# Four edits in the SSD stage of a four-layer convolution and state-space kernel: mask of the decays one slot earlier, pair scaling as one tensor-tensor operation, first convolution pass of B and C as scalar-tensor-tensor, turned B earlier

## The chip, the cores and the metric

The kernel runs on one core of one Trainium2 chip. A core has five engines with queues of their own: TensorE (PE in the profile, its weight loads PEld), VectorE (DVE), ScalarE (ACT), GpSimd (POOL) and SyncE (SP), which issues most transfers. The metric is the device time of one execution in microseconds, the median of several runs. All data are float32.

## The reference

An image batch x of shape (4, 96, 64, 64) goes through four layers one after the other. Layers 0 and 2 are selective-scan Mamba blocks with a fusion and a batch norm. Layer 3 is a 7x7 depthwise convolution with a layer norm and a two-layer perceptron. The change touches only layer 1, a state-space dual (SSD) layer:

```
xn = rmsnorm(x over channels) * norm_w
xs = four orders of the 4096 positions: rows, rows reversed, columns, columns reversed   # 16 sequences
z, xBC, dt = split(xs @ in_proj_w.T)              # 192, 192 + 128 + 128, 3
dt = softplus(dt + dt_bias)
xBC = silu(conv_b + causal 4-tap convolution of xBC along the sequence)
xh, B, C = split(xBC)                             # 3 heads of 64; 128 states
# by chunks; dAc = cumulative sum of dt * A in the chunk
y  = ((C B^T) * exp(dAc_s - dAc_t, s >= t) * dt) @ xh        # within the chunk
y += (C @ previous state) * exp(dAc)                         # what is carried in
state = exp(dAc_last) * state + (exp(dAc_last - dAc) * dt * xh)^T B
y  = rmsnorm((y + D * xh) * silu(z)) * gnorm_w
out = mean over the four orders of (y @ out_proj_w.T) + x
```

## The kernel before, in words

`program` runs the layers in order: `mamba_fusion`, `ssd`, `mamba_fusion`, `convnext`. The SSD stage is the class `Ssd`. For each of the 4 images it walks two orders (o: rows, columns) in two directions (r: forward, backward), and each of these 16 sequences in four blocks of 1024 positions (`BLK`), so there are 64 blocks. A block is eight chunks of 128 positions (`QB`, `Q`); there are 512 chunks.

`run` (L1401) is one loop over slots n, one slot for a chunk. In every slot each step is done for another chunk: `at(lag)` is the chunk n - lag, so `at(-4)` is four chunks ahead. What the steps are:

- `sums_to` (L1206) fetches, for a pair of chunks, the rows of cumulative decays from DRAM into dr, 128 times over the partitions, on SP.
- `mask_of` (L1219) adds a mask to dr on GpSimd and writes seg (128 x 3 x 128), for which there are six buffers. `decay` (L1227) takes three exponentials of seg on ScalarE. `weights` (L1240) multiplies seg by C B^T on VectorE.
- `inputs` (L1246) makes three scaled copies xs of x on GpSimd. `state` (L1266) multiplies xs by turned B on TensorE, `decayed` (L1275) scales the state before on GpSimd, and `update` (L1285) adds the two on VectorE.
- `carried` (L1294) and `within` (L1303) are the two matmuls that give y; `decayed_out` (L1311, VectorE), `skip` (L1320, GpSimd) and `gate` (L1324, VectorE) add them up and multiply by the gate z.
- `square` (L1334) and `scale` (L1339) make the inverse root mean square on ScalarE, for a pair of chunks in ssq. `scaled` (L1346) multiplies the pair yz by it on GpSimd, with two operations of 128 x 192. `by_channels`, `turned`, `project` and `finish` transpose the pair, project it and add it to the output X.

The projections and convolutions of a block are made by `front` (L1066), which returns a plan: a list of actions by age, four ages for a slot, begun 15 slots (`AHEAD`) before the block's first chunk. The first chunk's slot has age 60, and each slot calls the plan at four points (`fill(0)` to `fill(3)`), so two plans are usually under way. Actions of the plan:

- `channels` and `biased` (L1091, L1099): x by three matmuls with the convolution folded into the weights, and the bias added on VectorE.
- `project` (L1105), `begin` (L1116), `convolve` (L1126): B or C, whose bank in PSUM then goes through four passes on VectorE, one tap each. The first pass, in `begin`, multiplies by a tap and adds the bias with a tensor-scalar operation that has two scalars per partition. The three others are scalar-tensor-tensor operations that add to the tile.
- `gates` and `gated` (L1132, L1143): z on TensorE and its copy on ScalarE, made in the forward direction and kept for the backward one. z has five buffers.
- `silu_x` at age 36 and `silu_bc` at 46, on ScalarE, with a load of the activation table before and after.
- `turned` (L1161) and `kept` (L1170): B of four chunks transposed on TensorE and copied to bt on ScalarE; for chunks 0 to 3 at ages 56 and 57, for chunks 4 to 7 at ages 57 and 58. `state` of the block's first chunk is issued at age 58, after the plan's actions of age 57.

x, B and C, z, and the transposes of B share three PSUM banks ("front"). The order of the work on TensorE, VectorE, ScalarE and GpSimd is the order in which `run` writes it: L1529 to L1534 tie each instruction of a slot to the one before it on its engine. Only SP's order is left to the framework. Preludes of the next sequence are spread over the slots: for the row order `rmsnorm` (L888, work on all engines), for the column order `turn` (L941), which copies xn transposed on GpSimd, eight copies of 96 x 512.

Of the kernel before, what the change touches and what calls it, by code (L numbers as in the profile page):

```python
# [18 lines left out]
F32 = mybir.dt.float32  # L19
AF = mybir.ActivationFunctionType  # L20
ALU = mybir.AluOpType
# [5 lines left out]
L = HH * WW  # L27
P = 128
# [28 lines left out]
DI = 192  # L57
DST = 128
NH = 3
HD = 64  # L60
CONV = DI + 2 * DST
Q = 128
NQ = L // Q
BLK = 1024
QB = BLK // Q
# [242 lines left out]
class Scan:  # L308
# [118 lines left out]
    def keep(self, g, i):  # L427
# [3 lines left out]
        else:  # L431
            self.fuse(g, i, xs, self.po)

    def run(self, steps, wts, front, first, later):


# [16 lines left out]
        for n in range(-LEAD, total + 26):  # L453
            start = len(traced)
            if (n + LEAD) % each == 0 and (step := (n + LEAD) // each + 1) < len(steps):
                fronts.append((n, front(step, made[step])))
# [104 lines left out]
def mamba_fusion(ctx: ExitStack, tc, k, src, dst, w):  # L561
# [99 lines left out]
    for _ in front(0, made):  # L661
        pass
# [83 lines left out]
class Ssd:  # L746
# [141 lines left out]
    def rmsnorm(self, b):  # L888
# [36 lines left out]
        def stored(n, g):  # L925
            self.store_row(rows, n, g["pd"])

        stages = (load, None, affine, residual, squared, mean, root, scaled, row, stored)
        for m in range(4 * NT + len(stages)):
            for n, g in enumerate(items):  # L930
# [135 lines left out]
    def front(self, b, o, r, blk, made, following):  # L1066

        nc, k = self.nc, self.k
        xn = self.xn[o]
        base = blk * BLK
        plan = {}

        def at(age, what, *args):
            plan.setdefault(age, []).append((what, args))

        held = {}  # L1080

        order = range(QB) if r == 0 else range(QB - 1, -1, -1)

        def start():
            made["x"], made["bc"] = [], []
            if r == 1:
                made["z"] = self.z[blk]
            held["pk"] = self.pk
            self.pk = None

        def channels(m):  # L1091
            p = held["x", m] = self.bank("front")[:, :DI]
            for i in range(3):
                nc.tensor.matmul(  # L1094
                    p, lhsT=held["pk"][:, i, ds(order[m] * Q, Q)], rhs=self.conv[:, i],
                    start=(i == 0), stop=(i == 2),
                )

        def biased(m):  # L1099
            half, i = divmod(m, HALF_X)  # L1100
            if i == 0:
                made["x"].append(self.work.tile([P, HALF_X, DI], F32, name=f"x{half}"))
            nc.vector.tensor_tensor(made["x"][half][:, i], held.pop(("x", m)), self.xbias, ALU.add)

        def project(i):  # L1105
            q, (m0, m1) = i % 2, PARTS[i // 2]
            t0, n = min(order[m0], order[m1 - 1]) * Q, (m1 - m0) * Q
            p = self.bank("front")
            nc.tensor.matmul(
                p[:, : n + 3], lhsT=self.inw[:C, 2 * DI + q * DST : 2 * DI + (q + 1) * DST],  # L1110
                rhs=xn[:C, ds(base + t0 + (0 if r == 0 else PAD), n + 3)], start=True, stop=True,
            )
            shifts = [p[:, ds(tap if r == 0 else 3 - tap, n)] for tap in range(4)]
            held["bc", i] = n, shifts

        def begin(i):  # L1116
            q, (n, shifts) = i % 2, held["bc", i]
            if q == 0:
                made["bc"].append(self.work.tile([P, 2, n], F32, name=f"bc{i // 2}"))
            out = made["bc"][i // 2][:, q]  # L1120
            held["bc", i] = out, shifts
            nc.vector.tensor_scalar(
                out, shifts[3], self.taps[:, q, 3:4], self.bcbias[:, q : q + 1], ALU.mult, ALU.add
            )

        def convolve(i, tap):  # L1126
            q, (out, shifts) = i % 2, held["bc", i]
            nc.vector.scalar_tensor_tensor(  # L1128
                out, shifts[tap], self.taps[:, q, tap : tap + 1], out, ALU.mult, ALU.add
            )  # L1130

        def gates(c):  # L1132
            if c == 0:
                made["z"] = self.z[blk] = self.work.tile([P, QB, DI], F32, name="z", bufs=L // BLK + 1)
            p = held["z", c] = self.bank("front")[:, : 2 * DI]
            for i in range(2):
                nc.tensor.matmul(
                    p[:, i * DI : (i + 1) * DI],
                    lhsT=xn[:C, ds(PAD + base + (c + i) * Q, Q)], rhs=self.inw[:C, :DI],
                    start=True, stop=True,  # L1140
                )

        def gated(c):  # L1143
            z = made["z"][:, c : c + 2]
            nc.scalar.copy(z.rearrange("p c n -> p (c n)"), held.pop(("z", c)))

        def silu(tiles):
            for n, t in enumerate(tiles):
                k.act.other(t, t, AF.Silu, back=(n == len(tiles) - 1))

        def silu_x():
            silu(made["x"] + [made["z"]] * (r == 0))

        def silu_bc():
            silu(made["bc"])

        def load():
            if following and following[:2] in self.ready:
                self.pk = self.stack(*following[1:])

        def turned(m):  # L1161
            if m == 0:
                made["bt"] = self.work.tile([P, QB, DST], F32, name="bt")
            p = held["bt", m] = self.bank("front")
            for i in range(4):
                nc.tensor.transpose(
                    p[:, i * Q : (i + 1) * Q], self.part_of(made, r, m + i)[:, 0], k.ident
                )

        def kept(m):  # L1170
            bt = made["bt"][:, m : m + 4]
            nc.scalar.copy(bt.rearrange("p c n -> p (c n)"), held.pop(("bt", m)))

        at(0, start)
        for m, age in enumerate(XAGES):
            at(age + 1, biased, m)
        for i, age in enumerate(BCAGES):
            at(age + 1, begin, i)
            for tap in range(3):
                at(age + 2 + tap, convolve, i, tap)  # L1180
        if r == 0:
            for i, age in enumerate(ZAGES):
                at(age + 1, gated, 2 * i)
        for m, age in enumerate(XAGES):
            at(age, channels, m)
        for i, age in enumerate(BCAGES):
            at(age, project, i)
        if r == 0:
            for i, age in enumerate(ZAGES):
                at(age, gates, 2 * i)  # L1190
        at(24, load)
        at(36, silu_x)
        at(46, silu_bc)
        for m in (0, 4):
            at(57 + m // 4, kept, m)
            at(56 + m // 4, turned, m)
        return plan

    @staticmethod
# [18 lines left out]

    def mask_of(self, g):  # L1219

        seg = g["seg"] = self.work.tile([P, NH, Q], F32, name="seg", bufs=6)
        self.nc.gpsimd.tensor_tensor(  # L1222
            seg, g["pair"]["dr"][:, ds(g["c"] % 2 * NH, NH)],
            self.mask[:, g["r"]].to_broadcast([P, NH, Q]), ALU.add,
        )
# [120 lines left out]
    def scaled(self, g):  # L1346

        yz, ssq = g["pair"]["yz"], g["pair"]["ssq"]
        for n in range(2):
            self.nc.gpsimd.tensor_scalar(yz[:, n], yz[:, n], ssq[:, n : n + 1], None, ALU.mult)  # L1350

    def by_channels(self, g):

# [47 lines left out]
    def run(self):  # L1401
        nc = self.nc
# [5 lines left out]
        made = [{} for _ in steps]  # L1408
        chunks = []
        for n, (b, o, r, blk) in enumerate(steps):  # L1410
            for m in range(QB):
# [4 lines left out]
                    second=(m % 2 == 1),  # L1416
# [34 lines left out]
        for n in range(-8, len(chunks) + 7):  # L1451
            def at(lag):
                return chunks[n - lag] if 0 <= n - lag < len(chunks) else None
# [65 lines left out]
                self.update(g)  # L1519
            if g := at(0):  # L1520
                self.skip(g)
            if g := at(-4):
                self.mask_of(g)
            if (g := at(-6)) and not g["second"]:
                self.sums_to(g)
            fill(3)
            fronts = [f for f in fronts if f[1]]
# [356 lines left out]
```

## Time and profile before

| | |
|---|---|
| median of 3 runs (lowest, highest) | 8378.93 us (8374.79, 8385.31) |
| the profiled execution | 8395.19 us |
| its span | 8393.5 us |
| busy share of the span: PE, PEld, DVE, ACT, POOL | 86%, 38%, 90%, 62%, 83% |
| the SSD stage in it | 2773 to 5106 us, 2333 us |
| busy in that stage: PE, PEld, DVE, ACT, POOL | 2164.6, 1937.2, 2062.6, 1602.9, 1993.4 us |
| granted TensorE clock in that stage | 0.96 |

The span is that of the profiled execution on the device; its own time has 1.7 us around it. A group of the profile is written line, engine, operation, tiles and shapes, count, then busy time and mean of one instruction, then the idle time of its engine just before such instructions and who ended most of it ("<-POOL seg L1222": an instruction of line 1222 on GpSimd that wrote seg). Consecutive instructions of VectorE overlap by some 0.07 us in the trace, so busy times of groups add up to more than the busy time of the engine. The ends of matmuls are modelled.

### The profile page before, as it was taken

To read this page: it belongs to the slowest core of one execution; us is meant where nothing else is said; L and a number is where in the kernel's file an instruction comes from. 1 tells how busy PE (TensorE), PEld (TensorE's weight loads), DVE (VectorE), ACT (ScalarE), POOL (GpSimd) and SP (SyncE) were. 2 spreads that over 40 slices of the span, in tenths; PEclk is the share of its full clock that TensorE was granted. 3 is DMA by queue.
4 is the path that set the end of the run, shared out by engine and by line. 5 is a ranking of instruction groups with operands and counts; after the bars stand their busy time and mean duration, and the time that the engine had idled before them with its cause. 6 is when DMAs were issued, how large, how long until landed. Compare 5 with 4: busy or idle time off the path is not lost. (4 is left out here: it accounts for less than half of the span.)

```text
span 8393.5 us, 111634 instructions
## 1 busy us (share of the span) xinstructions
PE 7220.8 (86%) x33944; PEld 3213.4 (38%) x33944; DVE 7545.4 (90%) x8897; ACT 5240.3 (62%) x9510; POOL 6965.1 (83%) x4845
## 2 busy tenths in 40 slices
PE   7888888888886899999999997888888888888688
PEld 1222222222221787887888883222222222221122
DVE  6999999999997798898888895999999999999786
ACT  5666666666664677677677665566666656665255
POOL 5999999999997687887888886899999999999221
PEclk8999999999997999999999998899999999998799
DMA  7999989999896333333333325899999999998453
GB/s 183 239 238 253 233 236 254 237 244 247 230 242 176 101 95 104 102 94 106 103 97 108 90 86 135 228 239 246 248 235 250 240 235 243 234 244 231 114 128 76
DMA packets 819138, 1558.49 MB, mean 186 GB/s; under 512 B 117613, under 2 KB 123529, under 8 KB 815466
## 3 DMA queue, kind: packets, MB, share of 16 engines
q1 hardware_dynamic: 815466, 1546.23, 70.1%
q8 instruction: 272, 4.46, 0.2%
q10 hardware_dynamic: 3072, 5.11, 0.2%
q14 instruction: 328, 2.69, 0.1%
HBM read 1256.10 MB, written 148.50 MB: 167 GB/s over the span
## 5 line engine op out<-in xcount | busy, mean ns | idle before, releaser
L381 POOL TENSOR_TENSOR hc<-hs,bc 128x1024 f32<-128x1024 f32 x1536 | 3602.3, 2359 | 383.1 <-DVE hs L374 316.2
L374 DVE TENSOR_TENSOR_SCAN hs<-da,carry,bs 128x1024 f32<-128x1024 f32 x816 | 1914.7, 2346 | 120.0 <-issue 45.4
L346 PE MATMUL bs<-du,seldu 64*128 64x512 f32 x4352 | 1407.4, 691 | 654.4 <-DVE hs L374 648.3
L369 DVE TENSOR_TENSOR bs<-bs,bc 128x1024 f32<-128x1024 f32 x1088 | 1319.0, 1212 | 89.8 <-PE bs L346 71.7
L110 ACT ACTIVATE da<-da,w_a 128x1024 f32<-128x1024 f32 x1088 | 1230.6, 1140 | 5.2 <-DMA da<-dd 3.0
L354 POOL TENSOR_TENSOR du<-du,bc 128x1024 f32<-128x1024 f32 x448 | 1059.9, 2366 | 27.4 <-DMA du<-dg 27.4
L346 PEld LDWEIGHTS bs<-du,seldu 64*128 64x128 f32 x4352 | 394.5, 198 | 1625.6 <-issue 1143.4
L395 PE MATMUL py<-hc,selsum 128*32 128x512 f32 x6144 | 836.7, 615 | 37.8 <-DVE y L412 24.7
L110 ACT ACTIVATE bs<-da,w_a 128x1024 f32<-128x1024 f32 x448 | 500.2, 1116 | 542.4 <-DVE hs L374 267.5
L196 PE MATMUL pu<-h,w_conv 96*64 96x512 f32 (+1 forms) x3072 | 818.0, 653 | 7.8 <-ACT h L185 7.2
L110 ACT ACTIVATE seg<-seg,ndac 128x128 f32<-128x128 f32 x1536 | 502.9, 390 | 484.3 <-POOL seg L1222 477.2
L374 DVE TENSOR_TENSOR_SCAN hs<-bs,carry,du 128x1024 f32<-128x1024 f32 x336 | 781.2, 2325 | 0.6 <-ACT bs L110 0.6
L374 DVE TENSOR_TENSOR_SCAN hs<-da,bs 128x1024 f32<-128x1024 f32 x272 | 621.9, 2286 | 39.9 <-issue 15.7
L1128 DVE SCALAR_TENSOR_TENSOR bc<-front,taps,bc 128x384 f32<-128x384 f32 (+1 forms) x1152 | 648.3, 563 | 0.5
L1094 PE MATMUL front<-sconv,pk 128*128 128x192 f32 x3072 | 611.6, 337 | 7.1 <-DVE bc L1128 4.7
L1253 POOL TENSOR_TENSOR xs<-x,coef 128x576 f32<-128x576 f32 x512 | 590.5, 1153 | 25.3 <-DVE y L1331 25.3
L1322 POOL TENSOR_TENSOR y<-y,xs 128x192 f32<-128x192 f32 x496 | 294.1, 593 | 288.1 <-DVE y L1315 283.4
L1222 POOL TENSOR_TENSOR seg<-dr,mask 128x384 f32<-128x384 f32 x512 | 512.3, 1001 | 9.7 <-DMA dr<-rows 9.7
L1094 PEld LDWEIGHTS front<-sconv,pk 128*128 128x128 f32 x3072 | 511.0, 198 | 11.9 <-DVE bc L1128 4.2
L1676 DVE SCALAR_TENSOR_TENSOR acc<-strips,kern,acc 128x512 f32<-128x512 f32 x504 | 425.5, 846 | 51.1 <-ACT acc L1666 34.6
L115 ACT ACT_TABLE_LOAD x352 | 451.6, 1283 | 8.7 <-ACT dtrow L938 3.0
L122 ACT ACT_TABLE_LOAD x352 | 451.6, 1283 | 5.9
(225 smaller groups left out, 12765.6 us busy)
## 6 DMA issues: line engine op xcount, KB each, us to landing
da<-dd SPq DMA_DIRECT2D x3072, 256.0 KB
du<-dg SPq DMA_DIRECT2D x896, 256.0 KB
dr<-rows SPq DMA_DIRECT2D x256, 384.0 KB
bc<-rows SPq DMA_DIRECT2D x256, 256.0 KB
dd<-delta SPq DMA_DIRECT2D x192, 256.0 KB
dg<-du SPq DMA_DIRECT2D x192, 256.0 KB
pk<-xn SPq DMA_DIRECT2D x128, 384.0 KB
pk<-xn SPq DMA_DIRECT2D x128, 256.0 KB
```

Of the source, the lines that this page charges most:

```text
L110: self.last = self.scalar.activation(out, in_, func, **kw)
L196: nc.tensor.matmul(pu[HALFP * i : HALFP * (i + 1)], lhsT=wt["conv"][:kk, tap, D0[j] : D0[j] + HALFP], rhs=h[:kk, ds(i * T + tap, T)], star ...
L346: nc.tensor.matmul(g["bs"][:, i], lhsT=self.sel["du"][rows, g["half"], g["q"]], rhs=g["made"]["du"][rows, g["j"]], start=True, stop=True,)
L354: self.tc.nc.gpsimd.tensor_tensor(g["du"], g["du"], self.b_or_c(g, 0), ALU.mult)
L369: nc.vector.tensor_tensor(dbx, dbx, self.b_or_c(g, 0), ALU.mult)
L374: nc.vector.tensor_tensor_scan(out, da, dbx, init, ALU.mult, ALU.add)
L381: nc.gpsimd.tensor_tensor(g["hc"], hs, self.b_or_c(g, 1), ALU.mult)
L395: nc.tensor.matmul(py[ds(HALFP * i + QUART * x["half"], QUART)], lhsT=self.sel["sum"][:, q], rhs=x["hc"][:, i], start=(q == 0), stop=(q == ...
L1094: nc.tensor.matmul(p, lhsT=held["pk"][:, i, ds(order[m] * Q, Q)], rhs=self.conv[:, i], start=(i == 0), stop=(i == 2),)
L1128: nc.vector.scalar_tensor_tensor(out, shifts[tap], self.taps[:, q, tap : tap + 1], out, ALU.mult, ALU.add)
L1222: self.nc.gpsimd.tensor_tensor(seg, g["pair"]["dr"][:, ds(g["c"] % 2 * NH, NH)], self.mask[:, g["r"]].to_broadcast([P, NH, Q]), ALU.add,)
L1253: self.nc.gpsimd.tensor_tensor(xs, x.to_broadcast([P, 3, NH, HD]), coef.to_broadcast([P, 3, NH, HD]), ALU.mult)
```

## The change

It has four edits.

- `mask_of` is called for the chunk five ahead instead of four, and `sums_to` for the one seven ahead instead of six. seg has seven buffers instead of six. z has four buffers instead of five.
- `scaled` is one GpSimd tensor-tensor operation of 128 x 384, whose second operand is ssq broadcast along the channels, instead of two tensor-scalar operations of 128 x 192.
- `begin` is a scalar-tensor-tensor operation, whose added tensor is the bias broadcast along the positions, instead of a tensor-scalar one.
- The transposes of B for chunks 0 to 3 are at age 53 and their copy at 54; for chunks 4 to 7 at ages 56 and 57.

```diff
@@ begin
-            nc.vector.tensor_scalar(
-                out, shifts[3], self.taps[:, q, 3:4], self.bcbias[:, q : q + 1], ALU.mult, ALU.add
+            nc.vector.scalar_tensor_tensor(
+                out, shifts[3], self.taps[:, q, 3:4], self.bcbias[:, q : q + 1].to_broadcast([P, n]),
+                ALU.mult, ALU.add,
             )
@@ gates
-                made["z"] = self.z[blk] = self.work.tile([P, QB, DI], F32, name="z", bufs=L // BLK + 1)
+                made["z"] = self.z[blk] = self.work.tile([P, QB, DI], F32, name="z", bufs=L // BLK)
@@ the plan of front
-        for m in (0, 4):
-            at(57 + m // 4, kept, m)
-            at(56 + m // 4, turned, m)
+        for m, age in ((0, 53), (4, 56)):
+            at(age + 1, kept, m)
+            at(age, turned, m)
@@ mask_of
-        seg = g["seg"] = self.work.tile([P, NH, Q], F32, name="seg", bufs=6)
+        seg = g["seg"] = self.work.tile([P, NH, Q], F32, name="seg", bufs=7)
@@ scaled
-        for n in range(2):
-            self.nc.gpsimd.tensor_scalar(yz[:, n], yz[:, n], ssq[:, n : n + 1], None, ALU.mult)
+        self.nc.gpsimd.tensor_tensor(yz, yz, ssq[:, :, None].to_broadcast([P, 2, DI]), ALU.mult)
@@ run
-            if g := at(-4):
+            if g := at(-5):
                 self.mask_of(g)
-            if (g := at(-6)) and not g["second"]:
+            if (g := at(-7)) and not g["second"]:
                 self.sums_to(g)
```

## The prediction

> **What bounds the kernel now.** The diff touches only the SSD stage, 2773 to 5106 us of the span, so I read the groups of that stretch alone, first VectorE (line, operation, tiles, shape, count; then busy time, mean of one, idle time before it and what ended it):
>
> ```profile
> L1128 DVE SCALAR_TENSOR_TENSOR bc<-front,taps,bc 128x384 f32<-128x384 f32 x756 | 459.0, 607 | 0.2
> L1128 DVE SCALAR_TENSOR_TENSOR bc<-front,taps,bc 128x256 f32<-128x256 f32 x380 | 180.4, 475 | 0.1
> L1103 DVE TENSOR_TENSOR x<-front,xbias 128x192 f32<-128x192 f32 x504 | 176.3, 350 | 94.5 <-PE front L1094 92.1 <-POOL xs L1253 0.5
> L1331 DVE TENSOR_TENSOR y<-y 128x192 f32<-128x192 f32 x496 | 174.4, 352 | 31.4 <-POOL y L1322 30.1
> L1122 DVE TENSOR_SCALAR bc<-front,taps,bcbias 128x384 f32<-128x384 f32 x252 | 169.2, 672 | 27.5 <-PE front L1109 27.5
> L1292 DVE TENSOR_TENSOR prev<-prev,halves 128x192 f32<-128x192 f32 x480 | 164.9, 344 | 40.1 <-PE halves L1238 34.3 <-POOL seg L1222 2.1 <-POOL prev L1281 1.9
> ```
>
> The large groups have next to no idle time before them. VectorE's idle time in the stage, some 260 us of 2333, is what TensorE (92 + 34 + 27 here, 25 before X) and GpSimd (30) make it wait. So VectorE sets the pace and is stopped at a few places. GpSimd's groups:
>
> ```profile
> L1253 POOL TENSOR_TENSOR xs<-x,coef 128x576 f32<-128x576 f32 x512 | 590.5, 1153 | 25.3 <-DVE y L1331 25.3
> L1222 POOL TENSOR_TENSOR seg<-dr,mask 128x384 f32<-128x384 f32 x512 | 512.3, 1001 | 9.7 <-DMA dr<-rows 9.7
> L1350 POOL TENSOR_SCALAR yz<-yz,ssq 128x192 f32<-128x192 f32 x512 | 386.5, 766 | 3.1 <-ACT ssq L110 2.3 <-PE y L1307 0.8
> L1322 POOL TENSOR_TENSOR y<-y,xs 128x192 f32<-128x192 f32 x496 | 294.1, 593 | 288.1 <-DVE y L1315 283.4
> L1281 POOL TENSOR_TENSOR prev<-prev,dec 128x192 f32<-128x192 f32 x480 | 244.3, 509 | 18.8 <-DVE prev L1290 11.7 <-DVE prev L1292 6.8
> ```
>
> It is busy 85% of the stage but waits 283 us for VectorE's y, so mostly it follows. Three stretches of 33 us (length, then busy us and count of PE, PEld, DVE, ACT, POOL, granted clock, DMA) show that the bound changes:
>
> ```profile
> 3487.00:3520.00 33.00, 27.30 (x178) 24.16 (x177) 26.72 (x69) 20.89 (x56) 31.83 (x40) 0.98 0.28 84
> 3619.00:3652.00 33.00, 31.92 (x223) 30.19 (x222) 30.48 (x80) 23.59 (x59) 30.49 (x40) 1.00 0.31 97
> 3223.00:3256.00 33.00, 28.61 (x145) 22.70 (x143) 24.00 (x57) 24.14 (x51) 18.55 (x25) 0.84 0.37 112
> ```
>
> The second is a quiet block of eight slots (33.2 us from one turned-B copy to that of the next block). The first is a block that shares the engines with the turn of xn on GpSimd: blocks there take 39 to 40 us and GpSimd, at 31.83 of 33, is the bound. The third shares with the RMS norm of the next batch (46 to 48 us a block); no engine is full and the clock is down. Then the waits of the stage (who, for what, us, times, longest), and one block's end in order of time:
>
> ```profile
> ACT seg L110 <- POOL seg L1222: 477.2, 289, 3.7
> PE halves L1271 <- ACT bt L1172: 65.4, 53, 3.4
> ```
>
> ```profile
> 3623.46 0.99 ACT L110 ACTIVATE seg<-seg,ndac 128x128 f32<-128x128 f32 x3 [2.66 <-POOL seg L1222]
> ...
> 3624.70 0.56 ACT L1172 COPY bt<-front 128x512 f32<-128x512 f32 x1
> ...
> 3625.40 0.56 PE L1271 MATMUL halves<-xs,bt 128*128 128x192 f32 x2 [1.08 <-ACT bt L1172]
> ...
> 3626.29 0.35 DVE L1292 TENSOR_TENSOR prev<-prev,halves 128x192 f32<-128x192 f32 x1 [0.65 <-PE halves L1238]
> ...
> 3627.20 0.36 DVE L1103 TENSOR_TENSOR x<-front,xbias 128x192 f32<-128x192 f32 x1 [0.55 <-PE front L1094]
> ```
>
> This is the chain that matters: GpSimd's mask is late for ScalarE, so the decays, then the square, then the copy of turned B are late; the state matmul waits 1.08 us for that copy; VectorE loses 0.65 + 0.55. The transposes themselves ended near 3622.5, so the copy waited for its turn on ScalarE, not for data.
>
> **What the Trainium skill says.** "GPSIMD Engine Reference", section Elementwise — side-by-side cycle accounting, puts a two-input operation at about 2.6 cycles an element because both reads share one port, and section Engine selection calls one-input operations roughly line rate; by that the new two-input form would be no gain. The trace differs: y and mask (593 and 1001 ns for 192 and 384 elements) give 2.125 ns an element plus 185, which agrees, but the one-input L1350 takes 766 ns for 192, more than y. The measurement decides. "VectorE: DVE Perf Modes", section Why PSUM operands drop a tier, says that fp32 from PSUM runs at 1x; so the tensor-scalar form loses no faster mode. The trace agrees: from 256 to 384 elements both forms grow by about 1.04 ns an element, and differ by a constant. "Trainium Kernel Development and Optimization", section Best Practices, warns that matmul busy time is a bad metric and weight-load busy time a better one: PE's 93% is no proof of a bound, but 30.19 of 33 us of weight loads in the quiet block is a warning.
>
> **The change part by part.**
>
> *Turned B sooner.* The first four transposes go from age 56 to 53 and their copy from 57 to 54, of which the state matmul needs the result at 58; the other four go from 57 to 56, their copy from 58 to 57. Nothing is added: 8 transposes and 2 copies a block as before. The wait of 65.4 us should go. Its price on VectorE, from three quiet blocks (0.65+0.55, 0.65+0.62, 0.36+0.55) is 1.13 us per 1.08 of wait, so up to 65; I take 60, since in the crowded blocks (waits of 2.4 and 3.4 us) another stop would follow. What the moved transposes push back: about 0.5 us of TensorE, ahead of state, scores and channels in the slot at 3617 to 3621. There state's result was used 2.0 us after it was ready, and x (L1103, 3621.94) 1.0 us after channels ended at 3620.90; so it is hidden with 0.5 us to spare. They need silu of B and C, which ended at 3616.16, 3 us before. They also hold one of the three front banks until 54, so channels there waits for the copy of z (ended 3620.80, channels would start near 3620.3): 0 to 0.5 us in the 32 blocks that compute z. I take 5 us in all.
>
> *First pass as scalar-tensor-tensor.* 256 operations of 384 and 128 of 256: 672 - 607 = 65 ns and 536 - 475 = 61 ns less if the bias, as a stride-0 tensor, costs what the tap passes cost: 16.6 + 7.8 = 24 us. The form with a stride-0 operand is in the trace (L1315, 347 ns against 350 of L1103), so I keep 607. In a quiet block two of six are followed by a wait of 0.20 for X, where TensorE is late; so 16 us count. Ends: 0 (a form as slow as before) and 24; 40 ns dearer than before would cost 15.
>
> *A pair in one operation.* 512 x 766 ns become 256 of one. prev and xs, which also multiply by a stride-0 operand (509 and 1153 ns for 192 and 576), give 1.68 ns an element plus 187: 831 ns for 384; the mask, 1001, is the dear end. 2 x 766 - 831 = 0.70 us a pair, 180 us of GpSimd (136 at the dear end). Most is hidden, because GpSimd waits for VectorE's y anyway. It counts where y waits for GpSimd (30 us in all) and in the eight turn blocks where GpSimd is full: 4 pairs x 0.70 = 2.8 us each, 22 us; these overlap, and I take 30. The cheap cover is also needed: a block shortened to 31.7 us would leave GpSimd, at 30.5, no room without it.
>
> *Mask a slot sooner.* Same 512 masks in the same place of GpSimd's order, for a chunk one later, with a seventh seg buffer; the 256 transfers of dr are issued a slot sooner, some of them ahead of pk loads on SP that they followed; each still waits for the mask three pairs back, so what is queued behind it is held no longer than now, and GpSimd waited for dr once (9.7 us, at the start). z gets four buffers instead of five: a block's z is first written at least a slot after the last gate of a z that is dead by then, so no wait. ScalarE's 477 us of waits shrink, but ScalarE is busy 69% and, the turned-B chain apart, almost nothing waits for it; its square then waits for VectorE's yz instead. 5 us, in the norm blocks, where TensorE and VectorE wait for ScalarE's nsq.
>
> Sum: 60 + 16 + 30 + 5 - 5 = 106. From this I take 11 for TensorE: in quiet blocks it has 1.08 us of idle time, all of it the wait that goes, and its clock, 0.96 over the stage, may be granted less when it idles less. So -95: the profiled execution goes from 8395.2 to 8300, and the median, 16.3 below it now, from 8379 to 8284, 1.1% less.
>
> **The rivals.** *TensorE becomes the bound.* For: 31.92 of 33 us busy in the quiet block. Against: matmul ends are modelled, and VectorE ran there without a gap for slots on end. Then the first pass brings nothing and only about 35 of turned B and 15 of GpSimd remain: 8329. *GpSimd mattered more.* For: ScalarE's 477 us and the crowded blocks, where the waits chain; then its 180 us show by a third more and 145 us are gained: 8234. Against: 283 us of its own waiting. *No gain:* the time lost at turned B comes back at the next in-order wait: 8379; against it, VectorE's packed groups. *Slower.* One mechanism: the moved transposes hold the third front bank, so in every block channels on TensorE waits for ScalarE, whose z copy and turned-B copy come behind the square; VectorE's x then waits. It eats the whole gain at about 106 / 63 = 1.7 us a block; at 2.5 us the time is 8379 + 63 x 0.8 = 8429. For: more channels matmuls wait for ScalarE in the new program. Against: the copy of z above ended 0.5 us after the need at most, and ScalarE runs earlier, not later.
>
> **How the numbers follow.** Main case 0.6, TensorE 0.16, GpSimd more 0.08, no gain 0.06, slower 0.10. The main case alone spans 8250 to 8320: turned B 45 to 65, first pass 0 to 24, GpSimd 15 to 45. To hold 8 in 10 the range takes in TensorE's case and most of GpSimd's: 8230 to 8362. About 0.2% (17 us) is what a measurement of this kernel can tell from no change. Faster: 0.6 + 0.16 + 0.08 = 0.84, less 0.02 for the edge; same 0.07; slower 0.11.
>
> **What would show it.** Right: the state matmul no longer waits for bt; the wait of VectorE's prev for TensorE falls from 34 to under 10 us; the first pass at 607 and 475 ns; L1350 at 0.8 to 1.0 us; quiet blocks near 32 us and turn blocks near 37. Wrong: channels waiting for ScalarE by 1 us a block, x waiting for TensorE as long as now, a granted clock in the stage well under 0.96, or L1350 above 1.5 us.

## The result, and the profile after

| | before | after |
|---|---|---|
| median (lowest, highest) | 8381.08 us (8374.79, 8385.31) | 8291.53 us (8286.89, 8294.08) |
| profiled execution, its span | 8395.19, 8393.5 us | 8294.08, 8292.4 us |
| first to last gate of the SSD stage (start of the first and last yz on VectorE) | 2794.1 to 5099.7: 2305.6 us | 2795.0 to 4984.1: 2189.1 us |
| granted TensorE clock in the stage | 0.96 | 0.98 |

The ratio is 0.9893, 95% interval 0.9876 to 0.9910: 90 us less (75 to 104). Between the profiled executions it is 101 us: the SSD stage is 116.5 us shorter and what follows it 14.5 us longer, though no instruction of it was edited (the first 0.9 us is ahead of the stage). That second number comes back below.

VectorE's groups of the stage in the kernel after (2773 to 5010 us), those that answer to the groups shown of before; columns as there:

```profile
L1129 DVE SCALAR_TENSOR_TENSOR bc<-front,taps,bc 128x384 f32<-128x384 f32 x756 | 459.6, 608 | 0.2
...
L1103 DVE TENSOR_TENSOR x<-front,xbias 128x192 f32<-128x192 f32 x504 | 176.7, 351 | 51.1 <-PE front L1094 46.0 <-POOL xs L1254 1.1
L1332 DVE TENSOR_TENSOR y<-y 128x192 f32<-128x192 f32 x496 | 174.0, 351 | 17.0 <-POOL y L1323 16.9
...
L1293 DVE TENSOR_TENSOR prev<-prev,halves 128x192 f32<-128x192 f32 x480 | 164.7, 343 | 12.4 <-PE halves L1239 9.7 <-POOL prev L1282 1.9
L1122 DVE SCALAR_TENSOR_TENSOR bc<-front,taps,bcbias 128x384 f32<-128x384 f32 x252 | 153.9, 611 | 23.4 <-PE front L1109 23.4
...
L1122 DVE SCALAR_TENSOR_TENSOR bc<-front,taps,bcbias 128x256 f32<-128x256 f32 x126 | 60.0, 476 | 1.5 <-PE front L1109 1.5
```

VectorE's waits shrank where the prediction put them: idle time before x went from 94.5 to 51.1 us, prev from 40.1 to 12.4, y from 31.4 to 17.0. The first pass (L1122) costs 611 ns instead of 672. GpSimd's two groups that matter, same stretch:

```profile
L1323 POOL TENSOR_TENSOR y<-y,xs 128x192 f32<-128x192 f32 x496 | 294.3, 593 | 363.0 <-DVE y L1316 358.7
...
L1350 POOL TENSOR_TENSOR yz<-yz,ssq 128x384 f32<-128x384 f32 x256 | 211.8, 827 | 1.1 <-ACT ssq L110 1.1
```

The pair takes 827 ns; 386.5 us became 211.8, and GpSimd's own wait for VectorE's y grew from 283 to 359 us in a shorter stage: it follows VectorE still more. Three stretches of 33 us (length, busy us and count of PE, PEld, DVE, ACT, POOL, granted clock, DMA), a block with the turn of xn, a quiet one, one with the RMS norm:

```profile
3480.00:3513.00 33.00, 33.00 (x194) 24.57 (x194) 28.28 (x71) 24.01 (x60) 26.17 (x34) 1.00 0.34 97
3614.90:3647.90 33.00, 32.95 (x233) 31.39 (x233) 31.21 (x83) 25.39 (x68) 27.55 (x35) 1.00 0.37 105
3234.00:3267.00 33.00, 31.86 (x200) 26.93 (x199) 28.90 (x73) 23.08 (x55) 24.37 (x32) 0.97 0.39 111
```

GpSimd falls from 31.8 to 26.2 of 33 in the first; TensorE is recorded busy for 33.00 and 32.95 us in the first two. Whether that makes it the bound is asked below. In the third the granted clock is 0.97 where it was 0.84. The waits of the stage that answer to the two shown of before (who for what, us, times, longest):

```profile
ACT y L1338 <- DVE yz L1333: 475.7, 271, 5.3
...
PE front L1094 <- ACT z L1146: 11.8, 23, 0.7
```

ScalarE's decays no longer wait for GpSimd (477.2 us before); as predicted, its square waits for VectorE instead, 475.7 us where it was 173.0. The 65.4 us of the state matmul for turned B are gone; a wait of channels for the copy of z has grown from 2.3 to 11.8 us. The end of a quiet block:

```profile
3610.74 0.46 ACT L1146 COPY z<-front 128x384 f32<-128x384 f32 x1
...
3611.10 0.58 ACT L1173 COPY bt<-front 128x512 f32<-128x512 f32 x1
3611.25 1.24 PE L1094 MATMUL front<-sconv,pk 128*128 128x192 f32 x6 [0.38 <-ACT z L1146]
...
3615.23 0.55 PE L1272 MATMUL halves<-xs,bt 128*128 128x192 f32 x2
...
3617.01 0.36 DVE L1103 TENSOR_TENSOR x<-front,xbias 128x192 f32<-128x192 f32 x1 [0.36 <-PE front L1094]
```

The first copy of turned B starts 4.1 us ahead of the state matmul, where before the matmul waited 1.08 us for it. In return channels waits 0.38 us for the bank that the copy of z frees.

### The profile page after: what moved, and what is told of

It reads as the page before. It is cut to its first block, busy times and chain, and to the rows that moved or that the text cites. A ratio compares the mean times of both kernels' runs of the same rounds, so it can differ in the third digit from the quotient of the medians.

```text
span 8292.4 us, 111766 instructions
## 1 busy us (share of the span) xinstructions
PE 7184.2 (87%) x33944; PEld 3173.3 (38%) x33944; DVE 7523.9 (91%) x8897; ACT 5227.7 (63%) x9510; POOL 6788.3 (82%) x4589
## 5 line engine op out<-in xcount | busy, mean ns | idle before, releaser
L346 PE MATMUL bs<-du,seldu 64*128 64x512 f32 x4352 | 1420.8, 696 | 652.7 <-DVE hs L374 647.4
L346 PEld LDWEIGHTS bs<-du,seldu 64*128 64x128 f32 x4352 | 396.8, 199 | 1629.0 <-issue 1160.0
L196 PE MATMUL pu<-h,w_conv 96*64 96x512 f32 (+1 forms) x3072 | 824.1, 657 | 7.8 <-ACT h L185 7.2
L1094 PE MATMUL front<-sconv,pk 128*128 128x192 f32 x3072 | 596.3, 331 | 16.9 <-ACT z L1146 11.8
L1338 ACT ACTIVATE y<-yz 128x192 f32<-128x192 f32 x512 | 183.9, 359 | 548.2 <-DVE yz L1333 475.7
L1094 PEld LDWEIGHTS front<-sconv,pk 128*128 128x128 f32 x3072 | 493.8, 192 | 28.0 <-ACT z L1146 18.6
```

What stands on the lines that cost most here:

```text
L196: nc.tensor.matmul(pu[HALFP * i : HALFP * (i + 1)], lhsT=wt["conv"][:kk, tap, D0[j] : D0[j] + HALFP], rhs=h[:kk, ds(i * T + tap, T)], star ...
L346: nc.tensor.matmul(g["bs"][:, i], lhsT=self.sel["du"][rows, g["half"], g["q"]], rhs=g["made"]["du"][rows, g["j"]], start=True, stop=True,)
L1094: nc.tensor.matmul(p, lhsT=held["pk"][:, i, ds(order[m] * Q, Q)], rhs=self.conv[:, i], start=(i == 0), stop=(i == 2),)
```

## The experiments

Kernels of one set ran on the same chip beside runs of the kernel before; the sets ran on different chips, so ratios to before are compared, and converted to us with 8380. Beside each ratio stands the SSD stage of the profiled execution, first to last gate (before 2305.6), and the second Mamba stage, which follows it (first to last start of its scans on VectorE, before 2604.2). For each of these there is one execution a kernel. How far single executions differ shows in the first Mamba stage, which is the same program in all fourteen kernels and runs ahead of every edit: 2597.1 to 2618.1 us. A difference of stages under some 20 us is therefore not clear of one execution. The four quiet blocks of an image, 16 in all, are steadier: in most of the kernels they repeat within 0.1 us from image to image. A view of waits called "of the stage" below covers 2773 to 5000 us; where a stage ends later, the figure to its end is given too.

| kernel | ratio to before [95%] | us | SSD stage | second Mamba stage |
|---|---|---|---|---|
| after | 0.9893 [0.9876, 0.9910] | -90 | 2189.1 (-116.5) | 2620.7 |
| turned B alone | 0.9934 [0.9920, 0.9948] | -55 | 2258.1 (-47.5) | 2600.3 |
| mask alone | 0.9999 [0.9991, 1.0007] | -1 | 2287.7 (-17.9) | 2631.1 |
| pair alone | 0.9958 [0.9943, 0.9973] | -35 | 2271.1 (-34.5) | 2600.5 |
| first pass alone | 0.9984 [0.9973, 0.9994] | -13 | 2287.1 (-18.5) | 2589.4 |
| all but turned B | 0.9984 [0.9975, 0.9992] | -13 | 2266.5 (-39.1) | 2620.4 |
| all but mask | 0.9910 [0.9897, 0.9923] | -75 | 2232.2 (-73.4) | 2593.0 |
| all but pair | 0.9934 [0.9921, 0.9947] | -55 | 2214.0 (-91.6) | 2624.2 |
| all but first pass | 0.9912 [0.9899, 0.9926] | -74 | 2209.1 (-96.5) | 2627.3 |
| transposes at 55 and 68 | 0.9967 [0.9954, 0.9980] | -28 | 2255.3 (-50.3) | 2624.3 |
| the same, mask as before | 1.0148 [1.0133, 1.0163] | +124 | 2424.6 (+119.0) | 2607.6 |
| after, channels two matmuls of three | 0.9833 [0.9819, 0.9847] | -140 | 2156.3 (-149.3) | 2621.1 |
| after, B and C without a tap pass | 0.9801 [0.9785, 0.9816] | -167 | 2125.3 (-180.3) | 2610.4 |

Three theories stood against each other: that each edit gains what the sum of the prediction gave it; that TensorE bounds the stage once the wait is gone, so that VectorE's first pass brings nothing; and that GpSimd's time was the larger part of what is gained.

### Each edit alone, on the kernel before

Turned B:

```diff
-        for m in (0, 4):
-            at(57 + m // 4, kept, m)
-            at(56 + m // 4, turned, m)
+        for m, age in ((0, 53), (4, 56)):
+            at(age + 1, kept, m)
+            at(age, turned, m)
```

> The kernel before with turned B sooner alone (four transposes at age 53, their copy at 54). My theory: VectorE sets the pace and loses 1.13 us for each wait of the state matmul for bt, so 45 to 65 us less than before, and the wait of 65 us gone from the trace. Rival (the lost time comes back at the next in-order wait): under 15 us. Rival (channels waits for ScalarE behind the moved transposes): slower than before.

Measured: 55 us (44 to 67). The size is the predicted one, but not the place. From one block's copy of turned B to the next block's, the sixteen quiet blocks take 33.74 us on average instead of 33.34: they are slower. The two turn blocks of an image fall from 39.3 and 39.1 us to 36.5 and 36.5 (first image), and the last four blocks of the run, which are backward and compute no z, from 35.2, 32.7, 35.9 and 32.8 to 31.8, 31.3, 31.8 and 31.7. The waits of the stage (2773 to 5000 us) in this kernel say why:

```profile
ACT seg L110 <- POOL seg L1222: 491.7, 282, 4.0
...
PE front L1094 <- ACT z L1145: 45.8, 34, 2.2
```

Channels now waits 1.35 us, 34 times, for the front bank that the copy of z has to free (2.3 us in 3 waits before): as many times, within two, as there are blocks that compute z. Why that copy is late shows in one quiet block of this kernel in order of time:

```profile
3628.24 0.99 ACT L110 ACTIVATE seg<-seg,ndac 128x128 f32<-128x128 f32 x3 [2.15 <-POOL seg L1222]
...
3646.08 0.46 ACT L1145 COPY z<-front 128x384 f32<-128x384 f32 x1
...
3646.59 1.24 PE L1094 MATMUL front<-sconv,pk 128*128 128x192 f32 x6 [1.76 <-ACT z L1145]
...
3647.87 0.36 DVE L1103 TENSOR_TENSOR x<-front,xbias 128x192 f32<-128x192 f32 x1 [1.28 <-PE front L1094]
```

ScalarE waits 2.15 us for the mask just ahead of the two silus of the block, and from there on works without a gap for 18 us, through silus, table loads, decays and squares, until the copy of z. It doesn't catch up: channels waits 1.76 us for it and VectorE 1.28 for channels. In the same stretch of the kernel after ScalarE is early enough to wait 0.70 us for VectorE's yz on the way, and channels has no gap.

Mask:

```diff
-        seg = g["seg"] = self.work.tile([P, NH, Q], F32, name="seg", bufs=6)
+        seg = g["seg"] = self.work.tile([P, NH, Q], F32, name="seg", bufs=7)
-            if g := at(-4):
+            if g := at(-5):
                 self.mask_of(g)
-            if (g := at(-6)) and not g["second"]:
+            if (g := at(-7)) and not g["second"]:
                 self.sums_to(g)
```

and z with four buffers. The buffers were not tried apart from the earlier mask.

> The kernel before with the mask a slot sooner alone (seg 7 buffers, z 4). As predicted: about 5 us less than before. Second reading: the copy of turned B is late because the decays ahead of it on ScalarE wait for the mask; then the mask alone removes about half of each 1.08 us wait for bt and gives 25 to 40 us. The two edits then overlap, and the parts add up to more than the whole.

Measured: nothing in total (8 us less to 6 us more), and 17.9 us in the stage, which is not clear of one execution. The second reading, 25 to 40 us, failed. ScalarE's 477 us of waits for the mask change name; two waits of the stage in this kernel:

```profile
ACT y L1337 <- DVE yz L1332: 518.6, 238, 7.2
...
PE halves L1271 <- ACT bt L1172: 50.1, 48, 5.5
```

The state matmul still waits for turned B, 50.1 us to 5000 and 53.0 to the end of the stage (65.4 before): in one quiet block 0.65 us instead of 1.08, since the copy now comes behind the square only. The 18 us that the stage gains stand against 27 lost in the second Mamba stage (2631.1 against 2604.2 us).

Pair:

```diff
-        for n in range(2):
-            self.nc.gpsimd.tensor_scalar(yz[:, n], yz[:, n], ssq[:, n : n + 1], None, ALU.mult)
+        self.nc.gpsimd.tensor_tensor(yz, yz, ssq[:, :, None].to_broadcast([P, 2, DI]), ALU.mult)
```

> The kernel before with the pair scaled in one operation alone. As predicted: one operation takes 831 ns, and 15 to 45 us less than before, mostly in the eight blocks of the turn, which go from 39.5 to about 37 us. Rival (GpSimd only follows VectorE): under 8 us. Rival (GpSimd mattered more): over 60 us, since an earlier mask also makes the copy of turned B earlier.

Measured: 35 us (23 to 48), 34.5 in the stage. VectorE's y waits less for GpSimd (12.1 us over the stage, 30.1 before). The turn blocks gave less than predicted: together with the block after them 111.0 us instead of 113.0 (mean of four images), where turned B alone brings these three to 107.1. The window with GpSimd at 31.83 of 33 had made me call GpSimd their bound. The rest of the 34.5 is spread over all blocks in small parts; quiet ones take 33.02 us instead of 33.34.

First pass:

```diff
-            nc.vector.tensor_scalar(
-                out, shifts[3], self.taps[:, q, 3:4], self.bcbias[:, q : q + 1], ALU.mult, ALU.add
+            nc.vector.scalar_tensor_tensor(
+                out, shifts[3], self.taps[:, q, 3:4], self.bcbias[:, q : q + 1].to_broadcast([P, n]),
+                ALU.mult, ALU.add,
             )
```

> The kernel before with the first pass as scalar-tensor-tensor alone. As predicted: 607 and 475 ns an operation, 16 us less than before (24 if all of it counts). Rival (TensorE is the bound): within 5 us of before, with VectorE's waits for TensorE longer by what the passes save.

Measured: 13 us (5 to 23), 18.5 in the stage. That it brings nothing, as TensorE's theory had it, is just outside the interval. But the quiet blocks side with that theory: of the 0.38 us a block that VectorE saves (four passes at 65 ns, two at 61) they show 0.05, 33.29 us instead of 33.34. Of the stage's gain 13.9 us lie in the six blocks beside the RMS norms, whose three pairs differ by up to 5 us within this one execution.

### Each edit taken out of the kernel after

The same four pieces, undone one at a time:

```diff
@@ without turned B
-        for m, age in ((0, 53), (4, 56)):
-            at(age + 1, kept, m)
-            at(age, turned, m)
+        for m in (0, 4):
+            at(57 + m // 4, kept, m)
+            at(56 + m // 4, turned, m)
@@ without the mask (six seg and five z again)
-            if g := at(-5):
+            if g := at(-4):
                 self.mask_of(g)
-            if (g := at(-7)) and not g["second"]:
+            if (g := at(-6)) and not g["second"]:
@@ without the pair
-        self.nc.gpsimd.tensor_tensor(yz, yz, ssq[:, :, None].to_broadcast([P, 2, DI]), ALU.mult)
+        for n in range(2):
+            self.nc.gpsimd.tensor_scalar(yz[:, n], yz[:, n], ssq[:, n : n + 1], None, ALU.mult)
@@ without the first pass
-            nc.vector.scalar_tensor_tensor(
-                out, shifts[3], self.taps[:, q, 3:4], self.bcbias[:, q : q + 1].to_broadcast([P, n]),
-                ALU.mult, ALU.add,
+            nc.vector.tensor_scalar(
+                out, shifts[3], self.taps[:, q, 3:4], self.bcbias[:, q : q + 1], ALU.mult, ALU.add
             )
```

> The changed kernel with turned B put back (ages 56 and 57). My theory as predicted (turned B is worth 60 us whatever else is done): 45 to 65 us more than the changed kernel, so 25 to 45 us less than before. Second reading (mask and turned B overlap): only 15 to 35 us more than the changed kernel, 55 to 75 less than before.

> The changed kernel with the mask put back (four chunks ahead, seg 6 buffers, z 5). As predicted: 5 us more than the changed kernel. Rival (ScalarE's waits for the mask matter by themselves): over 15 us more.

> The changed kernel with the two tensor-scalar operations put back. As predicted: 30 us more than the changed kernel, in the turn blocks above all. Rival (GpSimd becomes the bound once VectorE is faster): over 45 us more, with y waiting for GpSimd in quiet blocks too. Rival (it only follows): under 8 us more.

> The changed kernel with the tensor-scalar first pass put back. As predicted: 16 us more than the changed kernel (24 if all of it counts). Rival (TensorE is the bound now that the wait for bt is gone): within 5 us of the changed kernel.

A difference of two of these ratios is known to about 18 us (half widths of 0.0013 and 0.0017, root of the sum of squares, by 8380). Taken out last, turned B is worth 76 us by the ratios (77 in the stage), more than both readings of it allowed, and the pair 34 (25). The first pass with 16 (20) and the mask with 14 are less than the ratios can tell, but the mask is worth 43 in the stage. So turned B and the mask are each worth more beside the other edits than alone, by 30 and 25 us in the stage. That it is these two that help each other is read from a wait; no kernel has these two alone. The wait, in the kernel without the mask edit:

```profile
PE front L1094 <- ACT z L1146: 47.3, 34, 2.5
```

It is 45.8 and 47.3 us in the two kernels with turned B sooner and the mask as before, 11.8 in the kernel after. VectorE's x waits 77.2 and 83.7 us for channels in those two, 46.0 after. Conversely, with all but turned B the state matmul waits 49.2 us over the stage for the copy, as with the pair alone (50.4). Quiet blocks take 32.58 us in the kernel after and 32.63 and 32.73 without the pair and without the first pass; without the mask they take 33.81, without turned B 32.88.

Other edits overlap. Mask, pair and first pass bring 17.9, 34.5 and 18.5 us of the stage alone, 70.9 in sum, but only 39.1 when all three are made without turned B; by the ratios it is 13 us of 49, a difference of 36 with an error of 18. So the four single figures, 118.4 us in the stage, add up to the 116.5 of the whole because this overlap and the help of turned B cancel.

### Can the bank be had without the wait?

The next block's plan runs 32 ages behind, so transposes at age 53 fall on its age 21: its gates have taken a bank at 20, which is free when the copy of z at 21 is done, and its channels want one at 22. If that coincidence were the whole cost, transposes at 55 and 68 (the next plan's 23 and 36, with no z nearby) should do better than the kernel after. The edit on the kernel after:

```diff
-        for m, age in ((0, 53), (4, 56)):
+        for m, age in ((0, 55), (4, 68)):
```

and the same with the mask as before; the first plan runs to age 71 at the start.

> The changed kernel with the transposes of B at ages 55 and 68 (copies at 56 and 69) instead of 53 and 56. At 55 the bank that the transposes take has been given up by z's copy long before, and VectorE, not ScalarE, frees the one that channels needs next. My theory (the moved transposes made channels wait for the copy of z): those waits, 12 to 19 us in the changed kernel, go, the state matmul still does not wait for bt, and 5 to 20 us less than the changed kernel. Rival (the waits are hidden): the same within 5 us.

> The same ages 55 and 68 with the mask put back (four chunks ahead, seg 6, z 5). My theory (the mask a slot sooner is worth something only because z's copy then comes before channels needs its bank): with that need gone the mask is worth nothing, and the time is within 6 us of the run with ages 55 and 68 alone. Rival (an earlier ScalarE is worth something by itself): 12 us or more slower than that run.

Both expectations failed. Ages 55 and 68 are 62 us slower than the kernel after. Two of its waits:

```profile
PE front L1109 <- ACT bt L1173: 33.4, 62, 1.7
...
ACT bt L1173 <- PE front L1167: 50.7, 55, 2.0
```

The wait of channels for z is gone (1.8 us), but now the projection of B or C, at age 24 next in line for a bank, waits for the copy of turned B (56, which is 24), once a block; and that copy, one age behind its transposes, itself waits for TensorE, so ScalarE stands idle for 50.7 us. In both places that were tried a bank is held until ScalarE gets to a copy, and somebody is in line for it. With the mask back at its old place, which was to cost nothing, the same kernel is another 152 us slower (waits to 5000 us of a stage that ends at 5222):

```profile
DVE prev L1293 <- PE halves L1239: 110.7, 65, 6.9
...
PE halves L1272 <- ACT bt L1173: 95.9, 43, 3.1
```

Here the copy is at age 56, two before its use and behind the decays of its slot; if those wait for the mask, the state matmul waits for the copy and VectorE's prev for that. The same mask edit is worth 18 us of the stage on the kernel before, 43 on the kernel after with turned B at 53 and 56, and 169 with it at 55 and 68.

### Which engine bounds the stage after

One kernel leaves out the third matmul of channels, 1008 matmul instructions in the trace, 156 us of TensorE by their group; the other leaves out the last tap pass of B and C, 375 operations; VectorE's busy time in the stage falls from 2049 to 1896 us.

```diff
@@ less TensorE: channels
-            for i in range(3):
+            for i in range(2):
@@ less VectorE: the plan of front
-            for tap in range(3):
+            for tap in range(2):
```

> The changed kernel without the third of the three matmuls of channels (the last part of x's convolution is left out): 512 times about 0.33 us of TensorE, 167 us, less, and none of VectorE's work. If VectorE sets the pace of the changed kernel: under 30 us less than the changed kernel. If TensorE has become the bound: over 80 us less.

> The changed kernel without the last tap pass of B and C (tap 2 of their convolution is left out): 256 passes of 0.53 us and 128 of 0.40 us by their starts, 187 us of VectorE, less, and none of TensorE's work. If VectorE sets the pace: 90 to 170 us less than the changed kernel. If TensorE has become the bound: under 30 us less.

Against the kernel after, less TensorE is 50 us faster by the ratios (33 in the stage), less VectorE 77 (64). Both lie between the forecasts of the two cases. So neither engine alone sets the stage: about a third or less of TensorE's 156 us shows, and half or less of VectorE's 153. The two are not quite alike, since with less TensorE its other matmuls got longer (those of L1308 from 268 to 270 ns) and its busy time fell by 101 us only. In the quiet blocks it is the other way round: 31.53 us with less TensorE and 31.88 with less VectorE, of 32.58, where each leaves out some 2.4 us a block. TensorE at 32.95 of 33 us busy was not the proof of a bound, and yet it counts for more there than VectorE. What VectorE's x waits for channels, in the kernel with less TensorE and then in that with less VectorE:

```profile
DVE x L1103 <- PE front L1094: 25.9, 30, 4.3
```

```profile
DVE x L1103 <- PE front L1094: 75.6, 148, 1.4
```

In the kernel after it is 46.0 us: with less work on one engine the other is waited for longer.

One thing moved in all these kernels that no edit aims at, the granted clock. In the traces it is either full or half, and half for 3.41 us or a multiple of that. From the first to the last gate TensorE ran at half clock for 157 us before, 86 with turned B alone, 143 with all but turned B, 48 after, 99 with less TensorE and 17 with less VectorE. Most such stretches go with a stop of TensorE: of its 27 stops of 1.6 us or more in the kernel before, 23 have one that begins in the stop or within 2.5 us after it, of its 118 stops of 0.3 to 1.6 us only 9. So an edit that takes away long stops seems to give back clock too. As an estimate from these figures, 109 us less at half clock are at most 55 us of the 116.5 that the stage gained; how much of it counts, no run here separates.

### The second Mamba stage

In the traces before and with the mask alone its instructions on VectorE, ScalarE and GpSimd and their order are the same. Still it takes 2610.4 to 2631.1 us in all eight kernels with the mask edit (mean 2622.4) and 2589.4 to 2607.6 in all six without (mean 2599.2; the kernel before is one of them): 23 us more, with no overlap. In the group of VectorE that grew, before and then with the mask alone (5178 to 7783 and 5161 to 7793 us):

```profile
L369 DVE TENSOR_TENSOR bs<-bs,bc 128x1024 f32<-128x1024 f32 x544 | 659.5, 1212 | 45.1 <-PE bs L346 39.4 <-remote 4.1
```

```profile
L369 DVE TENSOR_TENSOR bs<-bs,bc 128x1024 f32<-128x1024 f32 x544 | 660.1, 1213 | 68.6 <-PE bs L346 54.4 <-remote 12.7
```

VectorE waits longer for TensorE's L346, whose matmuls take 691 ns on average before and 699 after, and for something that the profile does not name ("remote"). L346 is not alone: TensorE's other large groups of this stage get longer too (L196 from 641 to 649 ns), and the granted clock of the stage is lower, 0.925 on average in the eight kernels and 0.937 in the six. Over all fourteen executions the stage is longer where its clock is lower, by some 16 us for 0.01. The first Mamba stage, ahead of every edit, goes the same way: 2597.1 us at a clock of 0.937, 2618.1 at 0.928, and on average 2607.4 us in the eight kernels and 2610.3 in the six. By that slope the lower clock goes with 20 of the 23 us; this is an estimate. What lowers the clock here after an edit in another stage is open. The mask edit gives ScalarE more separate wait instructions in the SSD stage (111634 instructions in the program before, 112044 with the mask alone); whether that has to do with it, no run here tried. What is shown is that the loss goes with the mask edit, lies outside the stage that was edited, and eats the gain of the mask alone.

## Why the prediction was right, and where it was not

- **The total.** 8284 was forecast, 8291.5 measured; for the profiled execution -95 and -101. Turned B (less its 5 us of bank waits), pair, first pass and mask were forecast at 55, 30, 16 and 5 us, and alone measured 55, 35, 13 and 1. That the sum holds for the whole is luck in part: in the stage the three other edits overlap by 32 us without turned B, and turned B is worth 30 more beside them than alone, and these two cancel.
- **Turned B.** "The wait of 65.4 us should go" held, and so did the size, 55 us alone. That its gain is read from the quiet blocks at 1.13 us each was wrong: alone it makes these slower by 0.4 us. The failing step is the pushing back: channels waits for the copy of z "0 to 0.5 us in the 32 blocks", 5 us in all. It was 1.35 us in 34 waits, 45.8 us. That figure came from a block of before in which the copy had ended early enough; once VectorE and TensorE no longer stop for turned B, ScalarE is the one behind, as the block shown above has it. The mechanism is that of the rival "slower", which decides at 1.7 us a block; alone, turned B came to 1.35 of it, and gained because the backward and turn blocks paid for it.
- **Mask.** That "the turned-B chain apart, almost nothing waits for it" was the other failing step, the same one seen from ScalarE: the copy of z waits for it too. In the stage the mask edit is worth 18 us alone (not clear of one execution) and 43 with the rest, not 5; the total shows 1 and 14, since the second Mamba stage is longer by some 23 with it. The two misses, turned B too cheap in bank waits and the mask worth too little, undo each other in the kernel after, where channels waits 11.8 us.
- **First pass.** 607 and 475 ns forecast, 611 and 476 measured; 16 us forecast, 13 (alone) and 16 (taken out last) measured. The place was wrong: the 16 were read from a quiet block, of whose 0.38 us two thirds were to count, and quiet blocks show 0.05 alone and 0.15 taken out last. The total came right by way of the crowded blocks, as far as one execution tells. The stride-0 operand costs what the tap passes' full one does.
- **Pair.** 831 ns forecast, 827 measured; 30 us forecast, 35 and 34 measured. The 22 of them that the turn blocks were to give were misplaced: with the block after them they gave 2.0 us a set of three, 8 us for four images, and 0.4 a set when the pair was taken out last (106.6 against 106.2). Busy 31.83 of 33 us was not the bound there, since turned B alone, which takes no work from GpSimd, shortens the set by 5.9. The two turn blocks were forecast near 37 us and came to 33.2 and 36.3 (second image), the block after them rising from 34.8 to 36.5.
- **TensorE becomes the bound** failed on its own test for the stage as a whole: the first pass alone brings 5 to 23 us, and 156 us less of TensorE bring 33 to 50. For the quiet blocks it was near the truth, as their 0.05 us shows. The 11 us taken off for TensorE can't be told apart from the errors, but their reason was wrong: TensorE's clock was to be granted less when it idles less, and it went up, from 0.96 to 0.98: the half-clock stretches lay beside long stops, and both became fewer.
- **GpSimd mattered more** failed too: without the pair edit GpSimd still has its 766 ns twice, and the kernel loses 34 us, not the 80 of that case (the 30 of the sum and 50 more).
- The Trainium skill, in "Trainium Kernel Development and Optimization", section Best Practices, says to judge how close a kernel is to its roofline by weight-load busy time (and the share of peak arithmetic) and not by matmul busy time. That page speaks of the roofline and not of what one edit gains; for the gain, this trace agrees that matmul busy time says little: 2111 of 2227 us busy, and a third or less of what is taken away shows. Weight-load busy time, 31.39 of 33 us in the quiet block, would not have told it either: there less than half of the 2.4 us left out shows.

## What to carry to other kernels

Where engines run in a written order and share a few banks, the price of moving one step is the wait of whoever is next in line for what the step holds, and it must be read with the other edits in place, not from the trace of before: the same mask edit was worth 18, 43 and 169 us of the stage. An engine that waits a lot and is "not the bound" (ScalarE, busy 69%) still matters at every copy that frees a bank behind its waits. Look at a steady stretch as well as at the total: the first pass gained what was forecast, but not in the blocks that the forecast was read from. Take edits out of the new kernel as well as putting them into the old one: only the pair of numbers shows which edits need each other and which overlap.

## What was not expected of the hardware

- A stage with the same instructions in the same order was 23 us (0.9%) longer in eight kernels than in six others, by an edit made elsewhere. Its granted clock was 0.925 instead of 0.937; what lowers it is open.
- The granted clock of TensorE went to half for 3.41 us or a multiple, beside 23 of its 27 stops of 1.6 us or more in the kernel before: 157 us of the stage, 48 after.
- TensorE recorded busy for 32.95 to 33.00 of 33 us still left room: over the stage, VectorE's time counts at least as much.
